# Four edits in a four-layer kernel: three of nine taps of the last convolution on GpSimd, layer norm's squares a step ahead, a fifth buffer of MLP weights, D's diagonals made by ScalarE

## The chip, the core and the metric

The kernel runs on one core of a Trainium2 chip. A core has TensorE (matmuls, results in PSUM), VectorE, ScalarE, GpSimd (which the profile calls POOL) and SyncE, whose queue issues every DMA of this kernel. The metric is the device time of one run in microseconds (us); lower is better.

## What is computed

Four layers with residuals and group norms, on 8 images of 384 channels and 32 x 32 pixels, all in fp32. Cut to what matters here:

```python
x = x + L0(gn(x))   # Mamba: in_proj, conv of 3, silu, x_proj, dt, scan over 1024 pixels, + u*D, * silu(z), out_proj
x = x + L1(gn(x))   # 1x1 conv, 8x8 FFT filter, depthwise 3x3, gelu gate, 1x1 conv
x = x + L2(gn(x))   # layer norm over channels, Mamba as L0, then an MLP 384 -> 1536 -> 384 with gelu
x = x + L3(gn(x))   # depthwise 3x3 conv with padding, one 3x3 filter per channel
```

In the scan, `h = exp(dt*A)*h + (dt*u)*B` and `y = sum_n h*C` for each of 768 inner channels and 16 states. In L3, each pixel is the sum of nine taps, each a shifted copy of the image times one number per channel.

## The kernel before, in words

**Chunks and steps.** An image is cut into two chunks of 512 pixels (`T`). There are 16 chunks for L0 and 16 for L2, worked through one after the other. A chunk has 24 steps (`NQ`), one for each 32 of the 768 inner channels. So there are 768 steps; steps 0 to 383 are those of L0 and steps 384 to 767 those of L2. A step `t` of the scan is:

- `begin` (three steps ahead): SyncE loads `dt*u` for this step from DRAM, spread over the 16 states, into a buffer `g` of four (L613).
- `times(t+1)`: GpSimd multiplies `g` by B, in two instructions (L623).
- `decay(t+1)`: TensorE spreads dt into four PSUM banks (`dA`), ScalarE takes the exponential.
- `scan(t)`: VectorE runs four scans (L643), multiplies two of the results by C (L654); GpSimd multiplies the other two by C in one instruction (L660).
- `gather(t-1)`: TensorE sums over states into `y`. After the last step of 128 channels, `u*D` is added, in L0 by a matmul with a diagonal matrix, in L2 by VectorE, and the result is multiplied by the gate.

**Jobs.** All other work is written as generators ("jobs") that are laid between the parts of the steps when the program is built: `front` (group norm, in L2 `layer_norm`, in_proj, x_proj, dt), `gates`, `measure` (statistics for group norm), `finish` (out_proj, in L2 the `mlp`), `layer1` and `layer3`. Each step gives the jobs a room of TensorE and VectorE time, counted by a meter that knows only columns (`ROOM`); a job that says `yield NEXT` goes on in the next step at the earliest. Each engine gets its instructions in the order in which they were recorded, and works through them in that order. Two places ignore the room: when `gates` of a chunk must be there (at the fifth and the seventeenth step of a chunk, `i % 12 == 4`), and when dt's result must be there, the program runs jobs by their due times until it is:

```python
        if i % (NH * NSUB) == NSUB:
            jobs.until(lambda: ("gates", i // (NH * NSUB)) in s)
```

**The last layer.** `layer3` runs once per image, when both chunks of it are through the MLP. For each of three blocks of 128 channels (`k`) ScalarE writes the normed image into `xp`, a buffer with a border of zeros, of which there is one. For each half `hf` of the image, `depthwise` adds nine taps in one PSUM bank: a matmul per tap, whose left side is a 128 x 128 diagonal matrix (`diag`, made by ScalarE from `eye`) and whose right side is a window of `xp`. The bank is then added to the residual by VectorE into `acc`, and SyncE writes `acc` out (L988). `acc` has one buffer, since its pool has `bufs=1`. I call the nine taps of one block and one half a group: 6 groups per image, 48 in all. An "image" below is counted from 0 to 7.

**Layer norm.** `layer_norm` runs once per chunk of L2. It sums the channels with three matmuls, subtracts the mean, and in a later step squares the three blocks on ScalarE (`sq`, in a tag `spm` of two buffers) and sums each square with a matmul into `ps_lv`. `spm` is also used by `measure` (pixels) and by dt (the softplus); a flag `live["spm"]` keeps `measure` and the others apart.

**The MLP's weights.** For each chunk the MLP uses 24 tiles `mw` of 384 KB: 6 for the first matmul and 6 for the second, for each half of the chunk. They lie in DRAM. Four buffers are filled ahead; the load of a further one is issued when the next tile is taken (`take`, `more`, L889).

**dt.** `step_dt` makes the softplus in `spm`, writes dt, multiplies dt by u on GpSimd into `du` (two buffers, L583) and writes it to DRAM with four DMAs (L590).

Of the kernel before, what the change touches and what calls it, by code (L numbers as in the profile page):

```python
# [10 lines left out]
F32 = mybir.dt.float32  # L11
# [144 lines left out]
def tile_conv_preact_d4(ctx: ExitStack, tc: tile.TileContext, a: dict, out: bass.AP):  # L156
# [10 lines left out]
    live = {"ps": 0, "dt": 0, "x": 0, "spm": False}  # L167
    work = [0.0, 0.0]
    jobs = Jobs(work)
    vector = Meter(nc.vector, work, 1)  # L170
# [182 lines left out]
        vector.tensor_scalar_mul(w["A"], w["A"], -1.0)  # L353
        return w

    def load_diagonal(w, pre):
        w["D"] = wk.tile([P, ND, P], F32, tag="w_D", name="w_D")
        nc.sync.dma_start(w["D"], a[pre + "D"].rearrange("d p q -> p d q"))

    def load_out(w, pre):  # L360
        w["out"] = wk.tile([P, ND, C], F32, tag="w_out", name="w_out")
        load_rows(w["out"], a[pre + "out_proj"], ND)

    def depthwise(pool, rows, todo):


        taps = [(n, t) for n in range(len(todo)) for t in range(9)]

        def diagonal(q):
            if q < len(taps):  # L370
                n, t = taps[q]
                d = pool.tile([P, rows], F32, tag="diag", name="diag", bufs=4)
                act(d[:rows], eye[:rows, :rows], AF.Copy, scale=todo[n][0][:, t : t + 1])
                return d[:rows]

        ready = deque(diagonal(q) for q in range(3))
        yield NEXT
        for q, (n, t) in enumerate(taps):
            if t == 0:
                ps = yield from ps_tile("ps_dw")  # L380
            _, window, take = todo[n]
            ready.append(diagonal(q + 3))
            mm(
                _img(ps[:rows]), ready.popleft(), window(t // 3, t % 3), start=t == 0,
                stop=t == 8,
            )
            if t == 8:
                take(ps[:rows])
                ps_done()
            if t % 3 == 2:  # L390
                yield
# [7 lines left out]
    def measure(s):  # L399

        blocks = [(h, k) for h in range(2) for k in range(KC)]
        loaded = {}

        def load(q):
            if q < len(blocks):
                h, k = blocks[q]
                x = loaded[h, k] = wk.tile([P, T], F32, tag="spm", name="xk", bufs=2)
                nc.sync.dma_start(
                    x, s["src"][s["b"], k * P : (k + 1) * P, h * T : (h + 1) * T]
                )  # L410

        live["spm"] = True
        load(0)
        load(1)
        yield NEXT

        def block(h, k):
            return loaded.pop((h, k)), lambda: load(blocks.index((h, k)) + 2)

        def all_read():  # L420
            live["spm"] = False

        s["stats"] = yield from group_stats(block, all_read, NEXT)

# [35 lines left out]
    def layer_norm(xn):  # L460
        ps = yield from ps_tile("ps_ln")
        for k in range(KC):
            mm(ps, ln_mean, xn[:, k, :], start=k == 0, stop=k == KC - 1)
        for k in range(KC):
            vector.tensor_sub(xn[:, k, :], xn[:, k, :], ps)
        ps_done()
        yield NEXT
        while live["spm"]:
            yield WAIT
        ps = yield from ps_tile("ps_lv")  # L470
        for k in range(KC):
            sq = wk.tile([P, T], F32, tag="spm", name="sq", bufs=2)
            act(sq, xn[:, k, :], AF.Square)
            mm(ps, ln_mean, sq, start=k == 0, stop=k == KC - 1)
        rsqrt(ps, ps, eps_ln)
        yield
        for k in range(KC):
            vector.scalar_tensor_tensor(
                xn[:, k, :], xn[:, k, :], ln_w[:, k : k + 1], ps, ALU.mult, ALU.mult
            )  # L480
        ps_done()
        yield NEXT
        for k in range(KC):
            act(xn[:, k, :], xn[:, k, :], AF.Identity, bias=ln_b[:, k : k + 1])
        yield NEXT

    def front(s):
# [78 lines left out]
        def step_dt(d):  # L566
            got = {}


            def log(ps):  # L570
                mm(ps, w["dt"][DT0:RX, d * P : (d + 1) * P], dbc[DT0:RX, :])
                v = got["m"] = wk.tile([P, T], F32, tag="spm", name="spm", bufs=2)
                act(v, ps, AF.Abs)
                act(v, v, AF.Exp, scale=-1.0)
                act(v, v, AF.Ln, bias=1.0)

            def plus(ps):
                v = s["dt"][d] = wk.tile([P, T], F32, tag="dt", name="dt", bufs=NDT)
                vector.scalar_tensor_tensor(v, ps, 0.0, got["m"], ALU.max, ALU.add)

            def times_u(ps):
                v = got["du"] = wk.tile([P, T], F32, tag="du", name="du", bufs=2)
                nc.gpsimd.tensor_mul(v, s["dt"][d], u[d])  # L583

            def spill(ps):
                to = s["dud"][d] = dram.tile(
                    [NSUB * E8, 4, T], F32, tag="dud", name="dud", bufs=2 * ND
                )
                for j in range(4):
                    nc.sync.dma_start(to[:, j, :], got["du"][32 * j : 32 * (j + 1), :])  # L590

            return [both(log, plus), None, both(times_u, spill)]

        yield from pipe([("ps_bc", [spread(j)]) for j in range(2)])
        yield
        flying = []
# [8 lines left out]
        while flying:  # L605
            flying = [f for f in flying if next(f, f) is not f]
            yield NEXT


    def begin(s, i):  # L610
# [53 lines left out]
    def gather(s, i):  # L664
# [208 lines left out]
    def weights():  # L873
# [21 lines left out]

# [74 lines left out]
    def layer3(s):  # L970
# [3 lines left out]
        for k in range(KC):  # L974
# [16 lines left out]
        live["x"] -= NCH  # L991


# [14 lines left out]
    load_diagonal(layer_w["l0_"], "l0_")  # L1008
    jobs.until(lambda: not jobs.jobs)
    load_out(layer_w["l0_"], "l0_")  # L1010
    for t in range(AHEAD):
# [167 lines left out]
```

## Time and profile before

| what | value |
|---|---|
| time, median of 3 runs | 7789.27 us (7788.77 to 7790.12) |
| the profiled execution's own time | 7774.96 us |
| its span in the profile | 7773.2 us |
| TensorE matmuls busy | 7244.1 us, 93% of the span |
| VectorE / ScalarE / GpSimd busy | 74% / 52% / 73% |
| first step of L2 (start of its L660) | 3560.6 us after the start |

The profile is of one execution. Busy time is the time in which an engine works on an instruction. "Idle before" a group of instructions is the time that the engine stood still just ahead of them, put down to what ended the wait. A matmul in fp32 shows as two records. Matmul ends are modelled[...].

### The profile page before, as it was taken

Reading aid. Unit: us, or ns where it says so; the run is one execution under the profiler, and the core shown is the slowest. Engines: PE = TensorE matmul, PEld = TensorE weight load, DVE = VectorE, ACT = ScalarE, POOL = GpSimd, SP = SyncE. Lnnn points to the kernel's source line nnn. Section 1 sums busy time; section 2 is a strip of 40 time slices with the busy share of each in tenths; the row PEclk is TensorE's granted clock in tenths of the full one; section 3 lists DMA queues with packets and bytes.
Section 4 is the critical chain, followed back from the end, with each engine's and each line's share of the span. In section 5 each row is a group of like instructions: output and inputs, shape, how many; then the busy total and the mean of one; then the engine's idle time right before and its main releaser. Section 6 shows DMA issues by size and latency. Waiting matters only on the chain. (4 is left out here: it accounts for less than half of the span.)

```text
span 7773.2 us, 76689 instructions
## 1 busy us (share of the span) xinstructions
PE 7244.1 (93%) x25762; PEld 3001.0 (39%) x25762; DVE 5787.0 (74%) x7350; ACT 4034.0 (52%) x6980; POOL 5638.8 (73%) x2710
## 2 busy tenths in 40 slices
PE   7989999999999999999999989999999999999998
PEld 2223333333333333333334434444444444444445
DVE  5988788888777878778746765767777677776871
ACT  4445555554554555455545544555555555555543
POOL 5888878788787878778646764767767677676770
PEclk8888889999888999988899999999999999999999
DMA  5666556556565646556536654666656666565662
GB/s 141 141 151 144 138 134 142 136 135 150 127 146 127 141 120 148 128 139 146 129 78 167 174 135 120 165 156 172 165 150 174 155 170 164 149 164 146 171 168 67
DMA packets 288919, 1122.50 MB, mean 144 GB/s; under 512 B 37386, under 2 KB 90970, under 8 KB 190220
## 3 DMA queue, kind: packets, MB, share of 16 engines
q1 hardware_dynamic: 288524, 1117.59, 58.4%
q8 instruction: 204, 3.34, 0.2%
q14 instruction: 191, 1.56, 0.1%
HBM read 1041.96 MB, written 75.50 MB: 144 GB/s over the span
## 5 line engine op out<-in xcount | busy, mean ns | idle before, releaser
L623 POOL TENSOR_TENSOR g<-g,bc 128x1024 f32<-128x1024 f32 x1536 | 3586.8, 2358 | 197.2 <-DMA g<-dud 181.2
L660 POOL TENSOR_TENSOR g<-g,bc 128x1024 f32<-128x1024 f32 x768 | 1806.2, 2352 | 1441.1 <-DVE carry L656 806.6
L241 ACT ACTIVATE dA<-dA,w_A 128x512 f32<-128x512 f32 x3072 | 1860.7, 662 | 1543.3 <-PE dA L177 1530.1
L177 PE MATMUL dA<-dt,selr 32*128 32x512 f32 x6144 | 1573.3, 677 | 70.6 <-DVE g L654 61.9
L643 DVE TENSOR_TENSOR_SCAN dA<-dA,carry,g 128x512 f32<-128x512 f32 x768 | 986.6, 1285 | 616.0 <-issue 275.6
L643 DVE TENSOR_TENSOR_SCAN dA<-dA,g 128x512 f32<-128x512 f32 x768 | 940.6, 1225 | 477.5 <-issue 167.7
L654 DVE TENSOR_TENSOR g<-dA,bc 128x512 f32<-128x512 f32 x1536 | 1053.9, 686 | 29.8 <-DVE dA L643 0.5
L177 PE MATMUL y<-g,sely 128*32 128x512 f32 x6144 | 934.1, 637 | 43.0 <-POOL g L660 37.5
L643 DVE TENSOR_TENSOR_SCAN g<-dA,carry,g 128x512 f32<-128x512 f32 x768 | 940.6, 1267 | 0.0
L643 DVE TENSOR_TENSOR_SCAN g<-dA,g 128x512 f32<-128x512 f32 x768 | 893.3, 1204 | 0.0
L177 PEld LDWEIGHTS dA<-dt,selr 32*128 32x128 f32 x6144 | 470.2, 191 | 984.4 <-DVE g L643 517.3
L177 PE MATMUL ps_dn<-h,mw 128*128 128x256 f32 x2304 | 573.9, 401 | 75.3 <-DMA mw<-in_l_mlp_w 58.6
L177 PE MATMUL ps_up<-t,mw 128*128 128x256 f32 x2304 | 566.8, 394 | 59.0 <-DMA mw<-in_l_mlp_w 44.2
L177 PE MATMUL ps_z<-xf,w_in 128*128 128x512 f32 x1152 | 586.1, 649 | 27.3 <-DVE dt L85 23.6
L177 PE MATMUL ps_in<-xf,w_in 128*128 128x512 f32 x1152 | 566.9, 633 | 27.3 <-DVE u L85 25.5
L177 PE MATMUL ps_dw<-tp,diag 96*96 96x512 f32 x1152 | 572.8, 638 | 15.2 <-ACT diag L241 15.2
L177 PE MATMUL ps_out<-u,w_out 128*128 128x512 f32 x1152 | 543.7, 619 | 10.2 <-DVE x L85 10.2
L177 PEld LDWEIGHTS ps_dn<-h,mw 128*128 128x128 f32 x2304 | 439.5, 197 | 277.0 <-issue 118.8
L177 PEld LDWEIGHTS ps_up<-t,mw 128*128 128x128 f32 x2304 | 425.8, 192 | 268.4 <-issue 148.9
L177 PE MATMUL ps_dw<-xp,diag 128*128 128x512 f32 x864 | 407.5, 622 | 42.2 <-ACT diag L241 40.9
L241 ACT ACTIVATE u<-ps_in,w_vec 128x512 f32<-128x512 f32 x192 | 149.4, 778 | 484.2 <-PE ps_in L177 484.2
L177 PEld LDWEIGHTS y<-g,sely 128*32 128x32 f32 x6144 | 134.2, 111 | 648.5 <-issue 461.1
(99 smaller groups left out, 6463.1 us busy)
## 6 DMA issues: line engine op xcount, KB each, us to landing
g<-dud SPq DMA_DIRECT2D x768, 1024.0 KB, 7.1
mw<-in_l_mlp_w SPq DMA_DIRECT2D x384, 384.0 KB, 7.4
dud<-du SPq DMA_DIRECT2D x768, 64.0 KB, 1.7
xk<-in_x SPq DMA_DIRECT2D x48, 256.0 KB, 4.2
xf<-in_x SPq DMA_DIRECT2D x16, 768.0 KB, 8.4
x<-in_x SPq DMA_DIRECT2D x16, 768.0 KB, 8.5
x_mid<-x SPq DMA_DIRECT2D x16, 768.0 KB, 4.6
xk<-x_mid SPq DMA_DIRECT2D x48, 256.0 KB, 5.0
```

Source lines behind the costliest of these rows:

```text
L177: nc.tensor.matmul(out_, lhsT, rhs, start=start, stop=stop)
L241: nc.scalar.activation(out_, in_, func, **kw)
L623: nc.gpsimd.tensor_mul(g, g, s["bc"][:, 0, :].unsqueeze(1).to_broadcast([P, 2, T]))
L643: nc.vector.tensor_tensor_scan(dAs[j] if j < own else g[:, j, :], dAs[j], g[:, j, :], 0.0 if s["c"] == 0 else carry[:, q : q + 1], ALU.mul ...
L654: nc.vector.tensor_mul(g[:, j, :], dAs[j], s["bc"][:, 1, :])
L660: nc.gpsimd.tensor_mul(g, g, s["bc"][:, 1, :].unsqueeze(1).to_broadcast([P, 4 - own, T]))
```

## The change

- **Taps.** `depthwise` gets a parameter `first`; for `layer3` it starts at tap 3. Taps 0, 1 and 2 are made by GpSimd: for each, a multiplication of a window of `xp` by one number per channel into `tap`, and an addition into `acc`, which starts from the residual. VectorE then adds the bank to `acc`. `tap` and `acc` have one buffer each.
- **Squares.** The three squares get three buffers of `spm` and are written in one piece; the matmuls follow in the next step. `live["spm"]` now holds the name of its user ("measure", "squares", "dt" or None), and each waits for the others.
- **Weights.** `mw` has five buffers, and five loads are issued at first.
- **D.** The diagonal matrices of D are no longer loaded (384 KB once); ScalarE makes each one from `eye` a step before its use, into a tile with one buffer.
- **dt.** `du` is gone: dt times u is written into the `spm` tile, which is thus held until the DMA to DRAM has read it; `spm` has three buffers. The loop over `d` in `front` goes on with the started ones while a new one can't start.

```diff
-    def load_diagonal(w, pre):
-        w["D"] = wk.tile([P, ND, P], F32, tag="w_D", name="w_D")
-        nc.sync.dma_start(w["D"], a[pre + "D"].rearrange("d p q -> p d q"))
...
-    def depthwise(pool, rows, todo):
-        taps = [(n, t) for n in range(len(todo)) for t in range(9)]
+    def depthwise(pool, rows, todo, first=0):
+        taps = [(n, t) for n in range(len(todo)) for t in range(first, 9)]
...
-            if t == 0:
+            if t == first:
                 ps = yield from ps_tile("ps_dw")
...
-                _img(ps[:rows]), ready.popleft(), window(t // 3, t % 3), start=t == 0,
+                _img(ps[:rows]), ready.popleft(), window(t // 3, t % 3), start=t == first,
...
-                x = loaded[h, k] = wk.tile([P, T], F32, tag="spm", name="xk", bufs=2)
+                x = loaded[h, k] = wk.tile([P, T], F32, tag="spm", name="xk", bufs=3)
...
-        live["spm"] = True
+        while live["spm"]:
+            yield WAIT
+        live["spm"] = "measure"
...
         while live["spm"]:
             yield WAIT
+        live["spm"] = "squares"
+        sq = [wk.tile([P, T], F32, tag="spm", name="sq", bufs=3) for _ in range(KC)]
+        for k in range(KC):
+            act(sq[k], xn[:, k, :], AF.Square)
+        yield NEXT
         ps = yield from ps_tile("ps_lv")
         for k in range(KC):
-            sq = wk.tile([P, T], F32, tag="spm", name="sq", bufs=2)
-            act(sq, xn[:, k, :], AF.Square)
-            mm(ps, ln_mean, sq, start=k == 0, stop=k == KC - 1)
+            mm(ps, ln_mean, sq[k], start=k == 0, stop=k == KC - 1)
+        live["spm"] = None
...
             def times_u(ps):
-                v = got["du"] = wk.tile([P, T], F32, tag="du", name="du", bufs=2)
-                nc.gpsimd.tensor_mul(v, s["dt"][d], u[d])
+                nc.gpsimd.tensor_mul(got["m"], s["dt"][d], u[d])
...
-                    nc.sync.dma_start(to[:, j, :], got["du"][32 * j : 32 * (j + 1), :])
+                    nc.sync.dma_start(to[:, j, :], got["m"][32 * j : 32 * (j + 1), :])
...
-        for d in range(ND):
-            while live["dt"] >= NDT or live["spm"]:
-                yield WAIT
-            live["dt"] += 1
-            flying.append(pipe([("ps_dt", step_dt(d))]))
-            flying = [f for f in flying if next(f, f) is not f]
-            yield NEXT
...
+        while d < ND or flying:
+            went = bool(flying)
+            if d < ND and live["dt"] < NDT and live["spm"] in (None, "dt"):
+                went = True
+                live["dt"] += 1
+                live["spm"] = "dt"
+                flying.append(pipe([("ps_dt", step_dt(d))]))
+                d += 1
             flying = [f for f in flying if next(f, f) is not f]
-            yield NEXT
+            if went and not flying:
+                live["spm"] = None
+            yield NEXT if went else WAIT
...
+        if sub == NSUB - 2 and s["pre"] == "l0_":
+            s["D", k] = wk.tile([P, P], F32, tag="D", name="D")
+            act(s["D", k], eye, AF.Copy, scale=s["w"]["vec"][:, k, 4:5])
...
-                mm(y, s["w"]["D"][:, k, :], u, start=False)
+                mm(y, s.pop(("D", k)), u, start=False)
...
-                w = p2.tile([P, NFH, P], F32, tag="mw", name="mw", bufs=4)
+                w = p2.tile([P, NFH, P], F32, tag="mw", name="mw", bufs=5)
...
-        for _ in range(4):
+        for _ in range(5):
             more()
...
+                acc = p2.tile([P, T], F32, tag="acc", name="acc")
+                so_far = x[hf][:, k, :]
+                for t in range(3):
+                    tap = p2.tile([P, T], F32, tag="tap", name="tap")
+                    nc.gpsimd.tensor_scalar_mul(_img(tap), window(0, t), dw3[:, k, t : t + 1])
+                    nc.gpsimd.tensor_add(acc, tap, so_far)
+                    so_far = acc
+
                 def take(ps):
-                    acc = p2.tile([P, T], F32, tag="acc", name="acc")
-                    vector.tensor_add(acc, ps, x[hf][:, k, :])
+                    vector.tensor_add(acc, ps, acc)
                     nc.sync.dma_start(out[b, k * P : (k + 1) * P, rows], acc)
 
-                yield from depthwise(p2, P, [(dw3[:, k, :], window, take)])
+                yield from depthwise(p2, P, [(dw3[:, k, :], window, take)], 3)
```

More of the change, by code (lines that the diff above doesn't have):

```diff
@@ L165, in tile_conv_preact_d4 @@
     psy = ctx.enter_context(tc.tile_pool(name="psy", bufs=1, space=PSUM))
-    live = {"ps": 0, "dt": 0, "x": 0, "spm": False}
+    live = {"ps": 0, "dt": 0, "x": 0, "spm": None}
     work = [0.0, 0.0]
@@ L420, in all_read @@
         def all_read():
-            live["spm"] = False
+            live["spm"] = None
         s["stats"] = yield from group_stats(block, all_read, NEXT)
@@ L571, in log @@
                 mm(ps, w["dt"][DT0:RX, d * P : (d + 1) * P], dbc[DT0:RX, :])
-                v = got["m"] = wk.tile([P, T], F32, tag="spm", name="spm", bufs=2)
+                v = got["m"] = wk.tile([P, T], F32, tag="spm", name="spm", bufs=3)
                 act(v, ps, AF.Abs)
@@ L595, in front @@
         yield
-        flying = []
-        for d in range(ND):
-            while live["dt"] >= NDT or live["spm"]:
-                yield WAIT
-            live["dt"] += 1
-            flying.append(pipe([("ps_dt", step_dt(d))]))
+        flying, d = [], 0
+        while d < ND or flying:
[6 more added lines that the diff above has]
+                d += 1
             flying = [f for f in flying if next(f, f) is not f]
-            yield NEXT
-        while flying:
-            flying = [f for f in flying if next(f, f) is not f]
-            yield NEXT
+            if went and not flying:
+                live["spm"] = None
+            yield NEXT if went else WAIT
     def begin(s, i):
@@ L1007, in tile_conv_preact_d4 @@
     jobs.until(lambda: ("gates", 0) in chunks[0])
-    load_diagonal(layer_w["l0_"], "l0_")
     jobs.until(lambda: not jobs.jobs)
```

## The prediction

> **What bounds the kernel now.** I read the busy shares and slices first, then the costliest groups with their idle time, then the waits by stage, then one stage in order of time.
>
> ```profile
> PE 7244.1 (93%) x25762; PEld 3001.0 (39%) x25762; DVE 5787.0 (74%) x7350; ACT 4034.0 (52%) x6980; POOL 5638.8 (73%) x2710
> ...
> PE   7989999999999999999999989999999999999998
> ...
> POOL 5888878788787878778646764767767677676770
> ```
>
> TensorE is the busiest in every slice, so a wait of TensorE costs time and a wait of another engine mostly doesn't. The groups by shape show which waits it has and what a GpSimd operation costs:
>
> ```profile
> L660 POOL TENSOR_TENSOR g<-g,bc 128x1024 f32<-128x1024 f32 x768 | 1806.2, 2352 | 1441.1 <-DVE carry L656 806.6 <-DVE g L643 616.4 <-DVE mv L85 15.6
> L177 PE MATMUL ps_dn<-h,mw 128*128 128x256 f32 x2304 | 573.9, 401 | 75.3 <-DMA mw<-in_l_mlp_w 58.6 <-ACT h L241 11.2 <-DVE dA L643 2.6
> L177 PE MATMUL ps_up<-t,mw 128*128 128x256 f32 x2304 | 566.8, 394 | 59.0 <-DMA mw<-in_l_mlp_w 44.2 <-DVE dt L85 5.5 <-ACT h L241 5.4
> L177 PE MATMUL ps_dw<-xp,diag 128*128 128x512 f32 x864 | 407.5, 622 | 42.2 <-ACT diag L241 40.9 <-ACT h L241 1.2
> L583 POOL TENSOR_TENSOR du<-dt,u 128x512 f32<-128x512 f32 x192 | 244.2, 1272 | 157.2 <-DVE dt L85 153.0 <-DMA dud<-du 4.2
> L177 PE MATMUL ps_lv<-sq,ln_mean 128*128 128x512 f32 x96 | 72.4, 915 | 40.2 <-ACT sq L241 40.2
> ```
>
> A step costs GpSimd 7.04 us (two L623, one L660) and TensorE at least 7.15 us; where it comes out at that, neither has room. The part that decides is the fifth step of a chunk, where the program runs what `layer3` has left. It looks like this in the order of time (TensorE's rows, then GpSimd's):
>
> ```profile
> 6657.10 10.57 PE L177 MATMUL ps_dw<-xp,diag 128*128 128x512 f32 x24
> 6668.86 15.72 PE L177 MATMUL ps_dw<-xp,diag 128*128 128x512 f32 x36 [1.20 <-ACT diag L241]
> 6684.42 5.31 PE L177 MATMUL ps_z<-xf,w_in 128*128 128x512 f32 x12
> ...
> 6658.65 4.66 POOL L623 TENSOR_TENSOR g<-g,bc 128x1024 f32<-128x1024 f32 x2
> 6691.76 2.36 POOL L660 TENSOR_TENSOR g<-g,bc 128x1024 f32<-128x1024 f32 x1 [28.45 <-DVE carry L656]
> ```
>
> 30 taps run alone on TensorE, GpSimd stands 28.45 us, VectorE waits for the banks, and the step takes 35.4 us. I call this a burst.
>
> [...]
>
> **The change part by part.** I also read the order of both programs' instructions, engine by engine. L0's steps 0 to 369 are unchanged but for D. In L2 the jobs fill each step as before; the saved taps come out of the bursts.
>
> *Squares.* 16 layer norms: 40.2 us idle, and 72.4 - 16 x 2.84 (six undisturbed records) = 27.0 us of stretch, 67 in all. The squares (637 ns each, 1.9 us) move to ScalarE's idle time a step earlier. Some of these steps then stop at what VectorE needs (6.9 us is the shortest step). I take -60, ends -67 and -30.
>
> *Weights.* 58.6 + 44.2 = 102.8 us. With a fifth buffer each load is issued where that of the tile ahead of it was. For each of the 59 waits I took the time between those two issues as the most that it can shrink: 85 us together. The 102.8 is the other bound. Loads take 7.4 us to land and share the DMA engines with 1 MB of `g` per step, so I take -68, ends -103 and -30.
>
> *Taps, TensorE.* 144 of 432 matmuls go: 18 took 15.72 us, so 0.873 each, 126 us. That isn't the gain. GpSimd gets 48 groups of three multiplications and three additions: 1.27 for an addition, 0.08 between dependent instructions (the gdv chain of group norm), and for the multiplication 0.53 (the rate of the xp memset: 1156 columns in 1.06 us) to 1.27. I take 0.8, so a group is 6.7 us.
>
> *Taps, bursts* (five images). 18 taps are left in each, 3 groups. `acc` has one buffer: group B's first addition waits for A's `take` (0.69) and its write to DRAM (2.0 from issue to landing). From the burst's start: GpSimd is free at 1.6, A is added at 8.2, taken at 9.0, written at 11.1. From there B needs 5.7 (its first multiplication is done by then: 1.27 and two of 2.2): added at 16.9, written at 19.7; likewise C is added at 25.4, taken at 26.2. VectorE's next scan stands behind C's `take` in its queue, and TensorE's next `dA` behind the scan: 7.3 us more (in before, 6685.23 to 6692.5). 33.5 instead of 35.5 us, though TensorE has only 17.6 us of work (0.92 of the 19.1 that the uncorrected columns give): -2 each, -10. Ends: -4 and +1.5 each.
>
> *Taps, first image.* Its burst (68.7 us) loses 21 taps, 9 of which go to other steps: 18 x 0.873 = -16; its two groups lie beside MLP matmuls.
>
> *Taps, spread groups.* 23 groups stand alone behind an L660. They delay the next L623 pair and the next L660, and then TensorE's `y`. Worked out at the same places of before's trace: L660 of step 287 of L2 ends at 6625.2; + 6.7 + 4.7 (L623 twice) + 2.35 = 6639.0; TensorE began that `y` at 6635.45: 3.6 us lost. Summed over the 23 places: +36 (0 where steps are long, 3.6 where short); at 0.53 it is +25, at 1.27 +56; since shorter steps have less room, up to +110.
>
> *Taps, tail.* The 18 taps left of image 6 after the last scan (15.72 and the diagonals, -17) move into the last steps, where three groups in a row make GpSimd the bound: 3 x 6.7 less some 3 us of idle, +17. Image 7 alone: 53 us before; six groups of 5.5 + 2.8 us are 50 to 52: -1.
>
> Sum of the taps: -10 - 16 + 36 - 1 = +9; ends -45 and +110.
>
> *D, dt, locks.* 96 activations of 0.40 us (the diag row) on ScalarE, 52% busy, a step ahead: 0; if they push exponentials back, +10. The 384 KB load lies ahead of the first scan, -3. The spm tile is held until the DMA read it (1.7 us), with three buffers and one dt a step: 0; if ScalarE waited there, the exponentials queue behind it and then VectorE's scans, +10.
>
> Sum: -60 - 68 + 9 = -119. Of the profiled execution, 7774.96 - 119 = 7656; the median lies 14.3 above it: 7670.
>
> **The rivals.**
> *Rival 1: the weights still wait.* SyncE's queue is in order, and loads stand behind DMAs that wait for GpSimd (dt's writes). For: one tile was issued 10.6 us after the matmul that freed its buffer began. Against: that issue lags by one block, and an extra tile is asked for ahead of it. -20 in place of -68: 7718. Chance 0.20.
> *Rival 2: the taps pay half.* If GpSimd runs ahead into the burst and writes land early, the bursts give -8 each and the spread groups cost 15: -40 - 16 + 15 - 1 = -42; total -170: 7619. For: GpSimd's median idle per step in L2 is 1.7 us. Against: the single `acc`. Chance 0.17.
> *Rival 3: slower, GpSimd becomes the bound behind each group.* Multiplication 1.27, a group 8.1 us; in 7.2 us steps 8.1 lies behind GpSimd's own 7.04 and all but some 1 us reaches `y`: 23 x 7 = 161, bursts +7, first image -16, tail +6: +158; with squares -50 and weights -50, +58: 7847. It decides from 4.5 us lost per spread group with these other terms (-103), from 6.7 with the forecast's (-155). Against: my places show at most 3.6 at 6.7. Chance 0.10.
> That the order of instructions doesn't change as said is excluded by the listing.
>
> **How the numbers follow.** The forecast's chance is 0.53: 7670. 0.2%, about what a measurement of this kernel can tell from no change, is 15.6 us: faster is below 7773.7. Forecast and rivals 1 and 2 hold 0.90; the upper ends of their unknown costs take 0.04 of that past the bound, half of it into no change: faster 0.86, same 0.03, slower 0.11. Range: -190 (rival 2 with a little more of the weights) to 0 (rival 1 with squares -30 and taps +50 or more): 7599 to 7789.
>
> **What would show it.** Right: ps_lv's idle near 0; mw's idle below 40 us; in a burst GpSimd works in three groups with waits of 2 to 3 us for `out<-acc`, and the step still takes over 30 us with TensorE idle about 12; `y` waits for L663. Wrong: bursts of 20 us, tap multiplications of 1.2 us or more, or mw's idle near 100.

## The result and the profile after

| what | before | after |
|---|---|---|
| time, median | 7789.02 us | 7976.95 us (4 runs, 7947.66 to 7994.02) |
| ratio, 95% interval | 1 | 1.0237 [1.0207, 1.0268] |
| the profiled execution's own time / span | 7774.96 / 7773.2 us | 7973.3 / 7971.3 us |
| granted TensorE clock, mean | 0.922 | 0.902 |
| first step of L2 / end of the last step of L2 | 3561 / 7590 us | 3576 / 7802 us |

The change makes the kernel 188 us slower. The forecast was 119 us faster. Every ratio below is of fast runs alone; one execution of `e9_one_tap` took 13047.9 us and is in none of them. The head of the page after, with the lines that answer to those shown of before:

```profile
PE 7241.7 (91%) x25474; PEld 3002.3 (38%) x25474; DVE 5789.6 (73%) x7350; ACT 3997.4 (50%) x6932; POOL 6038.6 (76%) x2998
...
PE   8989999999998999999999989888898898988987
...
POOL 5888888877887878777737767787777886778784
```

TensorE has 288 matmul records fewer and is busy for the same 7242 us, in a longer span: the second half of its row, nearly all nines before, now has many eights. GpSimd is busy 400 us longer. The same groups by shape as before, with the new ones (busy us, mean ns, then the idle time ahead of them and what ended it):

```profile
L177 PE MATMUL y<-g,sely 128*32 128x512 f32 x6144 | 988.7, 649 | 138.6 <-POOL g L663 135.1 <-DVE u L688 3.5
...
L177 PE MATMUL ps_dn<-h,mw 128*128 128x256 f32 x2304 | 599.0, 415 | 70.5 <-DMA mw<-in_l_mlp_w 43.4 <-DVE dt L85 14.2 <-ACT h L241 11.2
...
L177 PE MATMUL ps_in<-xf,w_in 128*128 128x512 f32 x1152 | 594.2, 658 | 94.6 <-DVE u L85 90.1 <-ACT dA L241 2.7 <-ACT xf L241 1.7
L177 PE MATMUL ps_up<-t,mw 128*128 128x256 f32 x2304 | 588.9, 405 | 46.9 <-ACT h L241 19.6 <-DMA mw<-in_l_mlp_w 16.1 <-ACT t L241 4.6
...
L997 POOL TENSOR_SCALAR tap<-xp,vec 128x512 f32<-128x512 f32 x144 | 225.0, 1563 | 36.9 <-ACT xp L241 25.8
...
L998 POOL TENSOR_TENSOR acc<-tap,x 128x512 f32<-128x512 f32 x48 | 60.8, 1266 | 63.2 <-DMA out<-acc 58.2 <-DVE dt L85 3.1
...
L177 PE MATMUL ps_lv<-sq,ln_mean 128*128 128x512 f32 x96 | 49.0, 649 | 0.0
```

Two of these rows were not shown of before. There they read:

```profile
L177 PE MATMUL y<-g,sely 128*32 128x512 f32 x6144 | 934.1, 637 | 43.0 <-POOL g L660 37.5 <-DVE u L681 5.3
...
L177 PE MATMUL ps_in<-xf,w_in 128*128 128x512 f32 x1152 | 566.9, 633 | 27.3 <-DVE u L85 25.5 <-ACT xf L241 1.7
```

Read from the bottom. The squares' wait is gone (0.0). A tap multiplication takes 1563 ns; the prediction took 800, gave 1270 as the upper end, and named 1.2 us or more as a sign of being wrong. The waits for `mw` are down from 102.8 to 59.5 us. `ps_in`, of which the prediction says nothing, now waits 90.1 us for VectorE's `u`; before it waited 25.5. That row was the first sign of a cause that I had not priced. And TensorE's `y` waits 135.1 us for GpSimd's last multiplication of a step, where it waited 37.5.

**Where in a stage the time lies.** I took the time from one L660 (after: L663) to the next, averaged over images 3 to 6 at the same one of an image's 48 steps. The burst (fifth step) went from 35.4 to 39.2 us. Steps 35 to 38 (counted from 0), where the second in_proj of an image's steps runs or has just run, went from 9.1, 9.1, 10.5 and 6.9 to 14.6, 15.5, 15.0 and 12.6; steps 30, 40 and 41 from 9.2, 8.3 and 8.6 to 15.9, 15.5 and 19.5. Others gained: step 11 (`ps_lv`) went from 13.2 to 9.2.

**The long in_proj steps** look like this on TensorE (start, length, instruction, in brackets the idle time ahead and what ended it):

```profile
6075.48 4.51 PE L177 MATMUL ps_in<-xf,w_in 128*128 128x512 f32 x6 [4.31 <-DVE u L85]
...
6082.58 2.81 PE L177 MATMUL ps_in<-xf,w_in 128*128 128x512 f32 x6 [1.52 <-DVE u L85]
...
6090.22 5.46 PE L177 MATMUL ps_in<-xf,w_in 128*128 128x512 f32 x6 [3.83 <-DVE u L85]
```

and on VectorE in the middle of it:

```profile
6080.90 1.53 DVE L85 SCALAR_TENSOR_TENSOR u<-ps_in,w_vec,u 128x511 f32<-128x511 f32 x2 [5.57 <-ACT xt L241]
6082.35 1.28 DVE L646 TENSOR_TENSOR_SCAN dA<-dA,carry,g 128x512 f32<-128x512 f32 x1
...
6088.56 1.51 DVE L85 SCALAR_TENSOR_TENSOR u<-ps_in,w_vec,u 128x511 f32<-128x511 f32 x2
```

A `ps_in` group needs one of three PSUM banks that all jobs share. TensorE goes on at 6082.58, and again at 6090.22, just when VectorE has read a bank (`u`, 6080.90 + 1.53 and 6088.56 + 1.51). VectorE reads `ps_in` behind the four scans in its queue, and for the next one stands 5.57 us (ScalarE's copy of a bank that TensorE has not filled yet). The two engines take turns. In before they don't, with the same instructions: what is different is that one of the three banks isn't there. In after, `layer3` puts the first three matmuls of a group into step 31 and the last three into step 41 of the order of instructions; the bank stays taken in between, and in each of images 2 to 6 all 36 `ps_in` records of that in_proj lie between the two halves. I call this the hold. In before the groups of these images lie elsewhere, and none is half done when in_proj runs (in image 1 one is, for 18 of the 36).

**The burst** is as the prediction drew it, but stretched. GpSimd in after:

```profile
6272.19 2.35 POOL L663 TENSOR_TENSOR g<-g,bc 128x1024 f32<-128x1024 f32 x1 [0.64 <-DVE carry L659]
...
6283.54 1.56 POOL L997 TENSOR_SCALAR tap<-xp,vec 128x512 f32<-128x512 f32 x1
6287.41 1.26 POOL L998 TENSOR_TENSOR acc<-tap,x 128x512 f32<-128x512 f32 x1 [2.31 <-DMA out<-acc]
...
6297.60 1.26 POOL L998 TENSOR_TENSOR acc<-tap,x 128x512 f32<-128x512 f32 x1 [1.25 <-DMA out<-acc]
```

Three groups with a wait for the store of `acc` between them, the last addition done at 6304.9, and the next L663 at 6311.97: 39.8 us after the last one, where 33.5 were forecast. Seven of the nine multiplications lie on this chain; the first of the second and of the third group is done while the store is awaited, since the additions behind them still wait 2.31 and 1.25 us. Seven at 0.76 us more than forecast are 5.3 us of the difference of 6.3. The first store adds about 1.1: from the end of its `take` (6284.17) to the addition 3.2 us pass, where the drawing had 2.1.

### The profile page after: what moved, and what is told of

It is laid out like the page before. It is cut to its first block, busy times and chain, and to the rows that moved or that the text cites. A ratio compares the mean times of both kernels' runs of the same rounds, so it can differ in the third digit from the quotient of the medians.

```text
span 7971.3 us, 76675 instructions
## 1 busy us (share of the span) xinstructions
PE 7241.7 (91%) x25474; PEld 3002.3 (38%) x25474; DVE 5789.6 (73%) x7350; ACT 3997.4 (50%) x6932; POOL 6038.6 (76%) x2998
## 5 line engine op out<-in xcount | busy, mean ns | idle before, releaser
L663 POOL TENSOR_TENSOR g<-g,bc 128x1024 f32<-128x1024 f32 x768 | 1804.2, 2349 | 1228.4 <-DVE g L646 619.9
L177 PE MATMUL dA<-dt,selr 32*128 32x512 f32 x6144 | 1557.0, 688 | 117.4 <-DVE g L657 109.9
L177 PE MATMUL y<-g,sely 128*32 128x512 f32 x6144 | 988.7, 649 | 138.6 <-POOL g L663 135.1
L177 PE MATMUL ps_in<-xf,w_in 128*128 128x512 f32 x1152 | 594.2, 658 | 94.6 <-DVE u L85 90.1
L177 PE MATMUL ps_dn<-h,mw 128*128 128x256 f32 x2304 | 599.0, 415 | 70.5 <-DMA mw<-in_l_mlp_w 43.4
L177 PE MATMUL ps_up<-t,mw 128*128 128x256 f32 x2304 | 588.9, 405 | 46.9 <-ACT h L241 19.6
L177 PEld LDWEIGHTS ps_dn<-h,mw 128*128 128x128 f32 x2304 | 461.3, 206 | 288.6 <-issue 136.0
L177 PEld LDWEIGHTS ps_up<-t,mw 128*128 128x128 f32 x2304 | 442.0, 200 | 266.5 <-issue 150.8
L85 DVE SCALAR_TENSOR_TENSOR u<-ps_in,w_vec,u 128x511 f32<-128x511 f32 (+1 forms) x384 | 282.3, 745 | 176.2 <-ACT xt L241 140.1
```

The source lines that it names most:

```text
L85: return call(out_, *args, **kw)
L177: nc.tensor.matmul(out_, lhsT, rhs, start=start, stop=stop)
L663: nc.gpsimd.tensor_mul(g, g, s["bc"][:, 1, :].unsqueeze(1).to_broadcast([P, 4 - own, T]))
```

## The experiments

Times of different series are compared by their ratio to the kernel before, which ran beside each; "of 7789" is that ratio times 7789 us. A "plus or minus" is worked out from the 95% intervals of the two ratios compared. Step times are of one profile each. The first four runs set two theories against each other. **Theory A**: all of the loss comes from GpSimd's tap work in front of its own work for the scan. **Theory B**: two costs, GpSimd's work and, apart from it, the bank held across in_proj.

| kernel | ratio to before | of 7789 |
|---|---|---|
| after | 1.0237 [1.0207, 1.0268] | 7974 |
| `e1_no_taps` | 1.0124 [1.0109, 1.0140] | 7885 |
| `e2_taps_d` | 1.0230 [1.0205, 1.0254] | 7968 |
| `e3_one_piece` | 1.0127 [1.0111, 1.0143] | 7888 |
| `e5_no_taps_guard` | 0.9903 [0.9871, 0.9934] | 7713 |
| `e6_d_loaded` | 0.9891 [0.9871, 0.9911] | 7704 |
| `e7_guard` | 1.0164 [1.0142, 1.0186] | 7917 |
| `e8_guard_no_gpsimd` | 0.9774 [0.9751, 0.9797] | 7613 |
| `e9_one_tap` | 0.9967 [0.9952, 0.9982] | 7763 |
| `e10_one_tap_acc2` | 0.9941 [0.9920, 0.9961] | 7743 |
| `e11_three_taps_acc2` | 1.0141 [1.0109, 1.0173] | 7899 |
| `e12_three_taps_mw4` | 1.0291 [1.0263, 1.0320] | 8016 |
| `e13_squares_late` | 0.9875 [0.9844, 0.9906] | 7692 |

### e1_no_taps: the changed kernel, all nine taps on TensorE

```diff
-                for t in range(3):
-                    tap = p2.tile([P, T], F32, tag="tap", name="tap")
-                    nc.gpsimd.tensor_scalar_mul(_img(tap), window(0, t), dw3[:, k, t : t + 1])
-                    nc.gpsimd.tensor_add(acc, tap, so_far)
...
-                    vector.tensor_add(acc, ps, acc)
+                    acc = p2.tile([P, T], F32, tag="acc", name="acc")
+                    vector.tensor_add(acc, ps, x[hf][:, k, :])
...
-                yield from depthwise(p2, P, [(dw3[:, k, :], window, take)], 3)
+                yield from depthwise(p2, P, [(dw3[:, k, :], window, take)])
```

> The changed kernel with all nine taps back on TensorE; squares, weights, D and dt as changed. Theory A (the whole loss is GpSimd's taps, and the other edits bring the 128 us that I forecast): 7660 us. Theory B (part of the loss is a PSUM bank: the new order starts a group of layer3 with three matmuls at the 32nd of 48 steps and ends it ten steps later, so in_proj between them has two banks in place of three; about 25 us in each of five images, with or without GpSimd's taps, since this kernel has the same order there): 7785 us, with TensorE still waiting for VectorE's u in the 36th to 38th step (14 to 16 us each, as in the changed kernel, 9 to 10.5 before).

Measured: 7875.13 us (7871.68 to 7878.85), against 7784.18 for before on the same chip. Both theories had it lower, but A had it faster than before, and it is 1.2% slower with no tap on GpSimd at all. A falls; B's figure was 90 us too low. The hold is still there in its order of instructions, the steps 35 to 38 take 15.4, 15.0, 15.1 and 13.0 us, and `ps_in` waits 92.3 us for `u`.

### e2_taps_d: the kernel before with GpSimd's taps and ScalarE's D, nothing else

```diff
+                acc = p2.tile([P, T], F32, tag="acc", name="acc")
+                so_far = x[hf][:, k, :]
+                for t in range(3):
...
+                    vector.tensor_add(acc, ps, acc)
...
+                yield from depthwise(p2, P, [(dw3[:, k, :], window, take)], 3)
...
+            act(s["D", k], eye, AF.Copy, scale=s["w"]["vec"][:, k, 4:5])
```

> The kernel before with GpSimd's three taps, and D made by ScalarE (without it the tap buffer has no room). Here layer3 keeps its old places and no group is held open over in_proj. Theory A: all of the 316 us between 7660 and 7977 is the taps: 8105 us. Theory B: 7977 - 7785 = about 190 us: 7980 us; steps 36 to 38 as before, the fifth step of a chunk about 39 us in place of 35.4.

Measured: 7956.35 us (7937.82 to 7978.44), 172 more than before. It has no hold in images 2 to 6 (steps 35 to 38 at 9.1, 9.1, 10.5 and 7.0), so here GpSimd's taps pay that, with D by ScalarE, which e6 below finds free within 29 us; 24 us from B's figure, 149 from A's.

### e3_one_piece: a group of the last layer is not cut in two

```diff
-            if t % 3 == 2:
+            if t == 8 or first == 0 and t % 3 == 2:
                 yield
```

> The changed kernel, but the six matmuls of a layer3 group are one piece, so that no bank is held from one step to another. GpSimd's work is the same. Theory A: 7977 us, as the changed kernel, within 20. Theory B: about 125 us less, 7850 us, and steps 36 to 38 at 9 to 10.5 us again.

Measured: 7877.95 us (7872.59 to 7882.01). With the six matmuls in one piece no bank is held between steps. Steps 35 to 38 are back at 9.1, 9.1, 10.5 and 6.9, and `ps_in` waits 17.0 us for `u`. By the ratios that is 86 us less than after; B had 127, A nothing. The group as a whole now lies in steps 40 and 41, so its place moved a little too.

### e5_no_taps_guard: e1 with a rule against the hold

```diff
+                while last and live["in"]:
+                    yield WAIT
+                live["dw"] = last
                 ps = yield from ps_tile("ps_dw")
...
                 ps_done()
+                live["dw"] = False
...
+        while live["dw"]:
+            yield WAIT
+        live["in"] = True
         yield from pipe(
             ("ps_in", [both(project(s, d, 0), tap(d), taps(d))]) for d in range(ND)
         )
+        live["in"] = False
```

> e1 (nine taps on TensorE, the other three edits) with a guard: a layer3 group doesn't begin while in_proj runs, and in_proj doesn't begin while a group is half done. Theory A: as e1. Theory B: about 125 us under e1, 7660 us; this would beat both kernels. If squares and weights brought nothing, 7789 us.

Measured: 7710.32 us (7676.39 to 7718.28), 165 us less than e1 on the same chip, with the same instructions in another order. Steps 35 to 38 take 8.2, 9.0, 9.6 and 9.1 us; `ps_in` waits 15.2 us for `u`. The rule also moves in_proj by two steps (it lies in steps 36 to 39, the last of which takes 9.1 us), and it is about in_proj alone: a group still lies half done over steps 30 to 36, while the MLP's `ps_up` runs. So the 165 us are the bank held over in_proj together with that move. The gain lies where the hold was: 157 of the 169 us by which the two profiles differ are in images 2 to 6, and in images 3 to 6 steps 35 to 41 become 36 us shorter. With e3, which removes the hold in another way, the cause is shown. The kernel also beats the one before.

### e7_guard and e8_guard_no_gpsimd: the taps without the hold, with and without GpSimd's part

`e7_guard` is the changed kernel with the rule of e5. `e8_guard_no_gpsimd` leaves three of the nine taps out of the output; TensorE's instructions and their order are those of e7. From e7 to e8:

```diff
-                for t in range(3):
-                    tap = p2.tile([P, T], F32, tag="tap", name="tap")
-                    nc.gpsimd.tensor_scalar_mul(_img(tap), window(0, t), dw3[:, k, t : t + 1])
-                    nc.gpsimd.tensor_add(acc, tap, so_far)
...
-                    vector.tensor_add(acc, ps, acc)
+                    vector.tensor_add(acc, ps, x[hf][:, k, :])
```

> The changed kernel with one rule more: a group of the last layer does not begin while in_proj runs, and in_proj does not begin while a group is half done. All taps by GpSimd, as in the change. Theory B (two separate costs: the held PSUM bank, and GpSimd's 8.5 us per group in front of its own work for the scan): the first goes, the second stays. The kernel with each group in one piece, which also had no bank held, took 7878, so 7880; steps 35 to 38 at 9 to 10 us, TensorE's waits for g (L663) still above 100 us. Rival A (the long steps came from the held bank alone, and GpSimd's taps cost by themselves no more than the 9 us of the prediction): 7713 (the kernel with nine taps and this rule, 0.9903 of the kernel before) plus about 10, less some gain, 7700 to 7725.

> As the last (six taps on TensorE and the rule for the last layer's groups), but GpSimd does none of its three taps: their sum is left out of the output, VectorE adds x as in the kernel before. It tells what TensorE's 192 x 0.655 us = 126 us are worth if GpSimd costs nothing, and its distance to the last kernel is the price of GpSimd's 288 instructions alone. If TensorE is the bound at the steps concerned (Theory B): 7713 - 100 = 7610, between 7590 and 7640. If those steps end on VectorE or ScalarE whatever TensorE does (rival C: the taps were never worth what TensorE saves): 7690 to 7715.

Measured on one chip: e7 7914.9 us (7892.18 to 7915.67), e8 7604.97 us (7594.77 to 7614.93). Theory B's figures for these were 7880 and 7610; rivals A and C fall. So 144 matmuls fewer are worth 100 us (e8 against e5, plus or minus 30): TensorE's gain was real, and its 126 us of busy time (144 x 0.873, which the expectation writes as 192 x 0.655) lie within that. GpSimd's 288 instructions cost 310 us, three times that. Where they go can be added up from two rows. GpSimd ahead of its last multiplication of a step, in e8:

```profile
POOL g L671 <- DVE carry L667: 680.3, 360, 45.6
POOL g L671 <- DVE g L654: 620.5, 262, 8.9
```

and in e7:

```profile
POOL g L671 <- DVE carry L667: 594.0, 352, 8.9
POOL g L671 <- DVE g L654: 491.4, 221, 8.3
...
POOL acc L1006 <- DMA out<-acc: 117.7, 22, 18.9
```

(total us, times, longest). GpSimd gained 404 us of work (6041.7 - 5637.5 busy) and 118 us of waiting for `acc`'s store, 522 in all. Its idle time ahead of L671 shrank by 215 us; the other 307 are the longer span (7913.9 - 7613.0 = 301). On TensorE's side `y` waits 212.3 us for L671 in e7 and 57.0 in e8, and `dA` waits 109.8 us for VectorE's L665 and 58.3.

One place shows how a group delays the scan. GpSimd in e7, at a step where two groups begin in two steps:

```profile
6156.51 2.35 POOL L671 TENSOR_TENSOR g<-g,bc 128x1024 f32<-128x1024 f32 x1
...
6169.79 1.27 POOL L1006 TENSOR_TENSOR acc<-tap,x 128x512 f32<-128x512 f32 x1 [8.16 <-DMA out<-acc]
...
6177.04 4.66 POOL L634 TENSOR_TENSOR g<-g,bc 128x1024 f32<-128x1024 f32 x2
6181.65 2.35 POOL L671 TENSOR_TENSOR g<-g,bc 128x1024 f32<-128x1024 f32 x1
```

SyncE's queue in the same stretch:

```profile
6160.11 1.73 SPq L599 DMA_DIRECT2D dud<-spm  x4
6161.95 0.53 SPq L624 DMA_DIRECT2D g<-dud  x1
6162.57 0.54 SPq L1011 DMA_DIRECT2D out<-acc  x1
```

VectorE had finished with the last group's `acc` at 6158.7. Its store stood in SyncE's queue behind dt's writes, which waited for GpSimd's own L592 (done at 6160.1), and behind a 1 MB load of `g`; it was issued at 6162.57 and had landed 7 us later. Then come 7 us of taps, and only then the two L634 and the L671 of the next step: 25.1 us from one L671 to the next instead of about 10 in e8. (This is step 46 of an image; after, whose groups lie elsewhere, has 11.1 there.)

### e9_one_tap: one tap of nine by GpSimd

```diff
-                for t in range(3):
+                for t in range(1):
...
-                yield from depthwise(p2, P, [(dw3[:, k, :], window, take)], 3, last=True)
+                yield from depthwise(p2, P, [(dw3[:, k, :], window, take)], 1, last=True)
```

> As the kernel with the rule, but one tap of nine by GpSimd (1.563 + 1.265 us per group, not 8.5), eight on TensorE. If GpSimd's cost is one of delay in proportion to its work (linear): a third of the way from 7713 to 7880, so 7770. If a short group fits into GpSimd's slack between two steps, and only what goes beyond it delays the scan (threshold, 4.5 us by the prediction's third rival): TensorE saves 48 x 0.655 = 31 us or a part of it, 7680 to 7705.

Measured: 7752.19 us, 7763 of 7789, near the linear forecast of 7770 and 50 us more than e5 (plus or minus 27). But the trace doesn't show GpSimd behind it (TensorE's waits in e9: total us, times, longest):

```profile
PE y L177 <- POOL g L671: 61.8, 39, 4.3
PE ps_up L177 <- ACT h L241: 36.0, 16, 2.7
```

TensorE's `y` waits for GpSimd no longer than in e5 (58.9 us); what grew is the wait of the MLP's `ps_up` for ScalarE, 3.5 us in e5. With eight matmuls to a group the order of instructions is another one: in each of images 2 to 6 a second group, beside that of steps 30 to 36, is half done while the MLP runs, from step 40 to step 46; e5, e7 and e8 have none there. Steps 42 to 46 together take 65.7 us in e9 and 46.7 in e5 (images 3 to 6). So e9 has a second bank held, which the rule doesn't exclude, and it can't tell the linear forecast from the threshold; what one tap costs GpSimd's own chain stays open.

### e6_d_loaded: e5 with D's matrix loaded again

```diff
-            s["D", k] = wk.tile([P, P], F32, tag="D", name="D")
-            act(s["D", k], eye, AF.Copy, scale=s["w"]["vec"][:, k, 4:5])
...
-                mm(y, s.pop(("D", k)), u, start=False)
+                mm(y, s["w"]["D"][:, k, :], u, start=False)
```

> The kernel with nine taps on TensorE and the rule for the last layer's groups (7713 when the kernel before takes 7789), with D's matrix loaded from DRAM again as in the kernel before; ScalarE does not make it. If ScalarE's 96 D instructions cost first-layer time (in every profile with them that layer's last step begins at 3574 to 3587, and at 3561 in the kernel before): 7698, and that step at about 3561. If they are free and the other edits account for those 13 us: 7713, and the step stays at 3574.

Measured: 7694.45 us, by the ratios 9 us below e5 (plus or minus 29). L2's first step begins at 3583 us in it, though ScalarE makes no D: the later start of L2 that I saw in after is not D's. In `e13_squares_late`, with D on ScalarE, it begins at 3557. Over all profiles that start lies between 3557 and 3587 us, for a reason that I did not find; D costs nothing that can be measured here.

### e10_one_tap_acc2, e11_three_taps_acc2, e12_three_taps_mw4: the single acc, and the fifth buffer

```diff
-                    acc = p2.tile([P, T], F32, tag="acc", name="acc")
+                    acc = p2.tile([P, T], F32, tag="acc", name="acc", bufs=2)
...
-                w = p2.tile([P, NFH, P], F32, tag="mw", name="mw", bufs=5)
+                w = p2.tile([P, NFH, P], F32, tag="mw", name="mw", bufs=4)
```

The first of these edits is in e10 and e11, the second in e11 and e12. e10 also makes its one product straight in `acc`, without `tap`.

> The kernel with one tap of nine by GpSimd (7763 when the kernel before takes 7789), with two buffers of acc in place of one acc and one tap buffer: GpSimd multiplies straight into acc and adds x in place. Its two instructions per group stay. Theory E (the one acc: GpSimd stood still for 104 us until out<-acc, the last group's store, had landed, with its own work for the scan queued behind): that wait goes, and with it most of the 83 us that one tap cost, so 7690; out<-acc ends no idle time of POOL. Rival F (GpSimd's 2.8 us of work per group cost the time, the waiting ran beside something else): 7750 to 7763.

> Three taps by GpSimd, the rule for the last layer's groups, two buffers of acc beside one tap buffer; four buffers of MLP weights, not five, to make room for it. To be read against the next kernel, which has one acc. Theory E: 118 us of GpSimd's idle time on out<-acc go, about 90 of them on the path: 90 less than the next, 7850 to 7880. Rival F: within 15 us of the next. In both, GpSimd's 8.5 us of work per group go on costing: it stays above the 7704 of the kernel without GpSimd's taps.

> Three taps by GpSimd, the rule for the last layer's groups, one acc (7917 with five weight buffers), with four buffers of MLP weights as in the kernel before. If the fifth buffer brings what its waits say (102.8 us of waits for mw with four, 60 to 76 with five): 7917 + 30 to 40, 7947 to 7957. If GpSimd's delays give the weights their time anyway: 7917 to 7925.

Measured on one chip: e10 7744.52 us, e11 7896.59 (7874.81 to 7917.07), e12 8017.61 (8000.40 to 8025.67). The first additions of GpSimd's groups in e12, then in e11:

```profile
L1006 POOL TENSOR_TENSOR acc<-tap,x 128x512 f32<-128x512 f32 x48 | 60.9, 1268 | 135.6 <-DMA out<-acc 124.6 <-DVE dA L654 7.7 <-DVE g L665 1.4
```

```profile
L1006 POOL TENSOR_TENSOR acc<-tap,x 128x512 f32<-128x512 f32 x48 | 61.0, 1270 | 4.2 <-DMA out<-acc 0.3
```

With three taps, the second `acc` takes away the wait for the store and 121 us of time: Theory E holds there, nearly one to one. With one tap it does not: of the 104.2 us of that wait in e9, 7.4 are left, the wait for `xp` grows from 10.6 to 46.5 us, and the time falls by 20 (plus or minus 20), by the ratios, close to Rival F. In e9 and e10 alike steps 42 to 46, with the second bank held, take 12 to 15 us each; probably the store's wait ran beside that. After the second `acc`, the work by itself still costs, as an estimate, 310 - 121 = 189 us, 3.9 us for each group's 8.5; the two numbers are of kernels with five and with four weight buffers.

e12 against e7 is the fifth weight buffer alone: 99 us (plus or minus 28), more than I expected for it. With four buffers the waits of `ps_dn` and `ps_up` for `mw` are 163.4 + 56.3 = 220 us, against 76 (52.8 + 23.4) in e7 with five.

### e13_squares_late: squares in the step of their matmul, the other order

```diff
         for k in range(KC):
             act(sq[k], xn[:, k, :], AF.Square)
-        yield NEXT
         ps = yield from ps_tile("ps_lv")
```

> The kernel with nine taps on TensorE and the rule (7713), with layer norm's squares not a step ahead: the one yield between the squares and the matmul that reads them is taken out. That puts the jobs back in the order of the kernel before, instruction by instruction on TensorE, in the steady part of the third layer; what is left of the change are five weight buffers, D by ScalarE and the locks. If the fifth buffer brings the 43 us by which the waits for mw fell: 7746, and the squares a step ahead are worth 33. If the squares account for the whole gain of 76 us: 7789. ps_lv's wait comes back, near 60 us.

Measured: 7686.63 us (7666.74 to 7725.62), 0.9875 of before: the lowest but for e8, and level with e6. Neither expectation holds: the squares a step ahead bring nothing that can be measured (22 us the wrong way, plus or minus 34), and weights, D and locks together bring 97 us (plus or minus 24). The rule is in e5 and e13 alike, but does different things there: in e13 in_proj stays in steps 34 to 36, as in before, and in e5 it moves to 36 to 39. Also, the group that is half done over `ps_up` in e5 (steps 30 to 36) is not so in e13. Both differences are part of the 22 us. The rows of e13:

```profile
L177 PE MATMUL ps_dn<-h,mw 128*128 128x256 f32 x2304 | 563.1, 398 | 30.1 <-DMA mw<-in_l_mlp_w 15.8 <-ACT h L241 11.2 <-ACT z L241 1.9
L177 PE MATMUL ps_up<-t,mw 128*128 128x256 f32 x2304 | 560.6, 393 | 33.7 <-DVE dt L85 22.8 <-DMA mw<-in_l_mlp_w 6.3 <-ACT h L241 3.5
...
L177 PE MATMUL ps_lv<-sq,ln_mean 128*128 128x512 f32 x96 | 69.2, 878 | 39.4 <-ACT sq L241 39.4
```

and of e5, where the squares are a step ahead:

```profile
L177 PE MATMUL ps_dn<-h,mw 128*128 128x256 f32 x2304 | 592.0, 410 | 62.5 <-DMA mw<-in_l_mlp_w 49.3 <-ACT h L241 11.2 <-ACT z L241 1.9
...
L177 PE MATMUL ps_up<-t,mw 128*128 128x256 f32 x2304 | 567.6, 395 | 25.4 <-DMA mw<-in_l_mlp_w 12.5 <-ACT t L241 4.0 <-ACT h L241 3.5
...
L177 PE MATMUL ps_lv<-sq,ln_mean 128*128 128x512 f32 x96 | 45.5, 610 | 0.0
```

The 39.4 us of `ps_lv` are exchanged for waits for `mw`: 22.1 us in e13, 61.8 in e5, and 50.6 in e6, which has TensorE's order of e5. The yield moves the jobs behind it by a step, and the weights are late again; that the MLP's matmuls come closer together is my reading, and no run tries it. The same move probably brings a group of `layer3` to step 31 and makes the hold: before and e2, without the squares' step and without the rule, have none in images 2 to 6. No run adds that yield alone.

## Why the prediction was wrong

From before to after, each row a difference of two ratios (in us of 7789):

| step | forecast | measured | from |
|---|---|---|---|
| fifth weight buffer, with D and locks | -68 | -97 ± 24 | e13 |
| squares a step ahead, no bank held | -60 | +22 ± 34 | e5 less e13 |
| the bank held over in_proj | 0 | +172 ± 27 | e1 less e5 |
| three taps to GpSimd | +9 | +88 ± 27 | after less e1 |
| sum | -119 | +185 | |

The last two rows depend on their order: taken the other way round, the taps cost 203 without the hold (e7 less e5) and the hold 57 with the taps (after less e7). Together they are 260 either way. The step times show why. Against after, e7 gains 32 us per image in steps 35 to 41, where the hold was, and 14 in steps 0 to 4 (images 3 to 6). But its rule sends two groups to steps 45 and 46, and steps 45 to 47 get 33 us longer. So the 57 is the hold less what the moved groups pay, and the 203 has that payment in it.

1. **"In L2 the jobs fill each step as before"** is the first of the two steps that failed. I read the order of instructions engine by engine for what it holds per step, and gave the move of `layer3`'s groups no price. I did not ask what a half-done group keeps while others run: one of three PSUM banks. With the same numbers of the same instructions, e1 takes 165 us more than e5.
2. **The sum of the taps, +9**, is the second: +88 with the hold, +203 without it, +179 in the order of before (e2, with D). The first thing wrong in it is the multiplication, 0.8 us with an end at 1.27: it took 1.563. I took the upper end from the two-input row and the lower from a memset; the 0.8 between them was an estimate, since all of GpSimd's rows in before are two-input operations or memsets. The one-input multiplication of a strided window by one number per channel (1.563) is dearer than the two-input addition (1.265); whether the window or the number per channel makes it so was not tried. A group is 8.5 us of work, not 6.7. With 1.563 in the prediction's own working, bursts are +17 (3.3 each; 3.8 measured, before to after) and spread groups about +69 (its 36 at 0.8 and 56 at 1.27 continued), the sum +69 with the other two terms. That lies within the +88 ± 27. By place it fits where most groups are: images 3 to 6 have four bursts and 12 lone groups, 49 us at these prices by estimate, and cost 53 (after less e1, one profile each); the last image with the end behind it cost 39, where the same estimate gives some 14. But these are prices in the order of after, and in other orders the same taps cost two to three times that (179, 203). In e7 the wait for the store of `acc`, 58.2 us in after, is 117.7, and a second buffer was worth 121 us (e12 less e11). The drawing of the burst was right.
3. **The squares**: the wait went as said (`ps_lv` at 0.0, its records from 915 to 649 ns), the time did not. The long records of before go with a lower clock and not with a wait inside them: its six `ps_lv` records at 6742.88 took 5.49 us at a granted clock of 0.50, those at 7235.31 took 2.97 us at 1.00, both after a wait of 3.0 us for `sq`. Of what is late next, I named only "what VectorE needs (6.9 us is the shortest step)"; the weights were, by 28 to 40 us of waits (e6 and e5 against e13).
4. **The weights**: right, and rather too small. In the order of before the waits fell from 102.8 to 22.1, by 81 us; the bound of 85 was nearer than the 68 that I took. The fifth buffer alone is worth 99 us where all three taps are GpSimd's (e12 less e7).
5. **D, dt, locks at nothing**: D by itself right within 29 us. dt and the locks were not tried apart.
6. **Rival 1** (the weights still wait) is in part what happened in after and e5 (59.5 and 61.8 us of waits), through the order of the jobs and not through dt's writes. **Rival 3** (GpSimd as the bound behind each group) came nearest to the mechanism of the taps, with a chance of 0.10: e7 less e8 is 6.5 us for each of 48 groups, where it asked for 7 in 23 places. Against it I had set that my places show at most 3.6 us, one group at a time. It left out the wait for the store of `acc`: 2.0 us in the prediction, which is the shortest that it took; in the place shown of e7, in a step that loads `g`, it was 7.0, after 4 us in SyncE's queue.

## What to carry to other kernels

An edit that changes where a job pauses, or how long its pieces are, moves everything behind it; e3 lost a held bank in that way, and e9 got one. Before pricing the edit, list what each half-done piece of work holds (a PSUM bank, a lock, a single buffer), and lay that span over the others' needs. Idle time of an engine inside a loop of waits (here GpSimd between VectorE's scans) is not room: of 522 us put there, only 215 were absorbed. A buffer that was written last and is now written first in a group makes the next group wait for the store of the one before (117.7 us in e7; a second buffer was worth 121 us, e12 less e11), on an engine whose own work for the scan is queued behind that wait. And a test with less of the work (here one tap) tests only that if the order of the rest stays as it was: compare the two orders first.

## What the runs showed of the hardware

TensorE's clock after short gaps. The six `ps_in` records (three matmuls) that took 2.81 us at 6082.58 took 5.46 us at 6090.22, after 3.8 us of idle time. Two windows of after (start and end, length, then the busy time of TensorE, its weight loads, VectorE, ScalarE and GpSimd, then the granted clock, the DMA share and GB/s):

```profile
6086.00:6090.00 4.00, 0.39 (x4) 0.00 (x0) 3.96 (x5) 0.27 (x2) 1.21 (x1) 0.89 0.60 156
6090.00:6092.00 2.00, 1.78 (x2) 0.84 (x3) 0.07 (x1) 0.00 (x0) 2.00 (x2) 0.50 0.96 213
```

The clock is 0.50 after nearly 4 us of idle time (0.39 us busy of 4), and stays there until about 6096 (0.51 from 6094 to 6096, 1.00 from 6096 to 6098). It does not fall after each gap of that length. I took the granted clock in the first microsecond after each idle gap of TensorE in after. It was one half (under 0.60) after all 21 gaps of 5 us and more, after 22 of 25 between 4 and 5, after 30 of 51 between 3 and 4, and after 12 of 60 between 1 and 2. A wait of about 4 us on TensorE thus can cost more than it shows, as longer matmuls: here some 2.65 us (5.46 - 2.81). Before has 19 and 7 gaps of the two longest kinds, after 25 and 21. That is probably part of why TensorE is as busy as before with 288 records fewer (mean granted clock 0.922 before, 0.902 after); no run separates it.
